# Attention with a sign-weight feed-forward: other places for the feed-forward's pieces, and one more product of ones in the first batch

## The chip, the core and the metric

The kernel runs on one core of a Trainium2 chip. Its engines work at the same time, each through its own list of instructions in order: TensorE (PE: matmuls and transposes, PEld: its loads of stationary weights), VectorE (DVE), ScalarE (ACT), GpSimd (POOL) and SyncE (SP, which here only issues DMAs). TensorE writes to PSUM, which is used as eight banks of 128 x 512 floats. The metric is the device time of one execution in microseconds. Before the change it is 4385.95 us, the median of three runs (4385.45 to 4386.15).

## The reference, cut to what matters

`x` is 4 batches of 2048 rows of 512 floats. There are 16 heads of 32 columns each.

```python
x = L0_attn_x
q, k, v = x @ Wq.T, x @ Wk.T, x @ Wv.T               # by head: (4, 16, 2048, 32)
attn = softmax(q @ k.T / sqrt(32), axis=-1)          # per head: 2048 x 2048
x = _layernorm(x + attn @ v)
w = where(weights >= 0, 1, -1)
y = clip((x @ w.T) * scale + bias, -100, 100)        # the feed-forward
x = _layernorm(x + y)
```

## The kernel before, in words

**Tiling.** Four heads (128 columns) are worked on together as one group: `n` counts the 16 groups, four per batch (`b, g = divmod(n, 4)`; `NG` is 4). In a group, `qb` counts four blocks of 512 queries (`NQB`), and `kc` counts 16 chunks of 128 keys (`NT`). One pair of block and chunk is one **step**: 64 steps per group (`STEPS`), 1024 steps in all (`total`). Batch 0 is the groups 0 to 3, and so on. I number steps of a group from 0 to 63; "step 11" without more means step 11 of the 16 steps of a block.

**One step on TensorE**, in this order:

- `scores`: for each of the four heads, a matmul that adds minus the row maximum (L300, bf16, with the tile `negm`) and one of keys by queries (L306), into four banks. ScalarE takes exp of the four banks into a tile `p` (L313), which comes from the pool `ppool` with four buffers.
- `max_unit`: queries by keys (L248) for a block 22 steps ahead (`LEAD`), into four banks. VectorE takes row maxima of three banks straight from PSUM; ScalarE copies the fourth to `moved` first. In the step named in `ahead` (step 11) VectorE also finishes the maxima of a block in `max_parts` (L280 to L284), between the first and second row maximum.
- **fillers**, from a plan (below).
- on even steps, `weighted`: exp times values for the two steps before (L324), which VectorE adds to `oT`.

GpSimd adds up the tiles `p` of a block in `acc` (`add_up`, L344): one addition for `kc` 1 to 14. When the block is over, `denominators` sums over keys with a matrix of ones (`ones_times`, L350): once with the last `p` (`kc` 15) and once with `acc`. The last block of all is treated otherwise (`is_last`).

**Fillers.** The order of all work is written out by the program that builds the kernel. `at(step, f)` puts a call at the end of a step (`behind`). `task(kind, first, last, f)` hands a piece of TensorE work to the planner, which places it between `first` and `last`:

- "big", on odd steps, at most two units of weight: `project_v` (a piece of values, weight 1), `project_k` and `project_q` (a piece of keys or queries, twice as wide, weight 2; all L206), and `ffn` (a third of the feed-forward of a tile of 128 rows, L532, weight 1, which VectorE works on in three instructions, L537, L538 and L540);
- "small", on odd steps: `transpose_x` (L195), `turn` (transposes of a normalised tile, L518) and `add_attention` (L391, two VectorE instructions on 512 columns);
- "col", on even steps: `denominators`.

`plan` walks through the steps. It takes the pieces whose `last` is near (`must`), then others (`can`) by their order of `last`. It runs twice: first as early as possible, to count how much weight falls in each group (`used`); then with these counts as `quota`, holding each group to its running share. A step is `heavy` when it is in `ahead` or has an `add_attention`; it then gets no third by choice, and no limit from the share. If one unit is allowed, a piece of values is preferred; if two, a third with a piece of values, or one wide piece.

**The feed-forward of a batch** runs beside the attention of the next. `finish(b, qb, a, every, w, lag)` sets its places for a block of 512 rows: load the rows (SP), statistics per tile of 128 rows (VectorE), `rstd` (a power on GpSimd) and `shift` (ScalarE), then for each of the four tiles, `every` steps apart, `norm` (ScalarE), a task `turn`, three tasks `ffn`; at last the second normalisation and the store (SP). `every` is 13 for the feed-forward of batches 0 and 1 and 11 for that of batch 2. That of batch 3 is placed by `finish_last` and `finish_end`, which are not touched.

Of the kernel before, what the change touches and what calls it, by code (L numbers as in the profile page):

```python
# [20 lines left out]
def kernel(  # L21
# [41 lines left out]
    kpool = ctx.enter_context(tc.tile_pool(name="kpool", bufs=2))  # L63
    qpool = ctx.enter_context(tc.tile_pool(name="qpool", bufs=3))
    vpool = ctx.enter_context(tc.tile_pool(name="vpool", bufs=2))
    ppool = ctx.enter_context(tc.tile_pool(name="ppool", bufs=4))
    apool = ctx.enter_context(tc.tile_pool(name="apool", bufs=2))
    work = ctx.enter_context(tc.tile_pool(name="work", bufs=2))
    once = ctx.enter_context(tc.tile_pool(name="once", bufs=1))
# [223 lines left out]
    def is_last(n, qb):  # L293
        return n == B * NG - 1 and qb == NQB - 1
# [22 lines left out]
    def weighted(pair):  # L317
# [18 lines left out]
            nc.vector.tensor_tensor(outs[n, qb], pb, outs[n, qb], ALU.add)  # L336
        give(b, "DVE", 0.6)

    def add_up(n, qb, kc, p, before):
        if kc == 1:  # L340
            acc[n, qb] = apool.tile([P, HG, QB], F32, tag="acc", name="acc")
        if 0 < kc < (NT // 2 if is_last(n, qb) else NT - 1):
            a = acc[n, qb]
            nc.gpsimd.tensor_tensor(a, before if kc == 1 else a, p, ALU.add)  # L344
        if kc == NT - 1:
            last_p[n, qb] = p

    def ones_times(b, p, start, stop):
        for h in range(HG):
# [17 lines left out]
    def denominators(n, qb):  # L367

        if is_last(n, qb):
            b = sums[0]  # L370
        else:
            b = take()
            ones_times(b, last_p.pop((n, qb)), True, False)
            whole = acc.pop((n, qb))
            ones_times(b, whole, False, True)
        if is_last(n, qb):
            dT = mpool.tile([P, QB], F32, tag="moved", name="dT")
        else:
# [195 lines left out]
    def at(step, f, *args):  # L574
        behind[step].append(lambda: f(*args))
# [2 lines left out]
        tasks[kind].append((last, first, len(tasks[kind]), f, args, after, gap))  # L578
        return kind, len(tasks[kind]) - 1

    def finish(b, qb, a, every, w, lag):
        f = Finish(b, qb)
        at(a, f.load)
        for j in range(NTQ):
            at(a + 2 + j, f.stats, 1, j)
        at(a + 6, f.rstd, 1)
        at(a + 7 + lag, f.shift, 1)
        for j in range(NTQ):
            t = a + 8 + lag + every * j
            at(t, f.norm, 1, j)  # L590
            turned = task("small", t + 1, t + 3, f.turn, j)
            for k in range(3):
                task("big", t + 2, t + w, f.ffn, j, k, after=turned)
            at(t + w, f.stats, 2, j)
        e = a + 9 + lag + every * (NTQ - 1) + w
        at(e, f.rstd, 2)
        at(e + 1 + lag, f.shift, 2)
        for j in range(NTQ):
            at(e + 2 + lag + j, f.norm, 2, j)
        at(e + 5 + lag, f.store)  # L600

    def finish_last(qb, last):

# [56 lines left out]
    for n in range(N):  # L660
        b, g = divmod(n, NG)
        s0 = n * STEPS
        ready = [s0 - STEPS + 1] * NQB
        for i in range(NQB):
            if g:
                break
            first = start if n == 0 else s0 - STEPS + (2, 10, 20, 31)[i]
            last = -LEAD + NTQ * i - (2 if i else 6) if n == 0 else first + (12, 12, 11, 8)[i]
            for j in range(NTQ):
                turned[b, i, j] = task("small", first, last, transpose_x, b, i, j)  # L670
            ready[i] = first
        def latest(i, s):

            return min(s, s0 + (0, 9, 19, 30)[i]) if g == NG - 1 else s

        for t in range(NT):
            i, j = divmod(t, NTQ)
            after = turned[b, i, j]
            task("big", max(s0 - STEPS + 2, ready[i], -6), latest(i, s0 + t), project_v, n, t,
                 after=after)  # L680
            if j % 2 == 0:
                continue
            free = s0 - STEPS + 1 if n else start
            task("big", max(free, ready[i]), s0 - LEAD - 1 + i * (1 if n else NTQ),
                 project_k, n, t // 2, after=after)
            last = s0 + NT * i - LEAD + NTQ * (j - 1) - 1
            if n == 0 and i == 0:
                last = -LEAD - 2 + j
            task("big", max(s0 + NT * (i - 2), start), latest(i, last), project_q, n, t // 2,
                 after=after)  # L690
        for qb in range(NQB):
            first = s0 + NT * qb
            last = first + NT - 1
            ahead[first - 5] = n, qb
            at(last + 2, load_columns, n, qb)
            w = 0 if n == N - 1 else 6
            d = last + 2 if is_last(n, qb) else last + 3
            t = task("col", d, d + w, denominators, n, qb)
            if is_last(n, qb):
                t = task("small", d + 1, d + 1, reciprocals, n, qb, after=t)  # L700
                task("small", d + 2, d + 2, add_attention, n, qb, after=t)
            else:
                task("small", d + 3, d + 4 + w, add_attention, n, qb, after=t, gap=3)
            if g == NG - 1:
                if b < B - 1:
                    every = 13 if b < B - 2 else 11
                    finish(b, qb, (b + 1) * NG * STEPS + qb * (5 * every - 1), every, every, 3)
                else:
                    (finish_end if is_last(n, qb) else finish_last)(qb, last)

# [6 lines left out]
    def plan(quota=None):  # L717

        gone = {kind: set() for kind in tasks}
        done, steps, used = {}, defaultdict(list), defaultdict(int)  # L720

        def may(kind, s):
            some = (t for t in tasks[kind] if t[1] <= s and t[2] not in gone[kind])
            return [t for t in some if t[5] is None or done.get(t[5], s) + t[6] <= s]

        s = start
        while any(len(gone[kind]) < len(tasks[kind]) for kind in tasks):
            middle = 0 <= s < total
            soon = s + 2 if 0 <= s + 1 < total else s + 1
            group, at_n = divmod(s, STEPS)  # L730
            if not middle:
                most = {"col": 1, "small": 1, "big": 1}
            elif s % 2:
                most = {"small": 1, "big": 2}
            else:
                most = {"col": 1}
            heavy = s in ahead
            for kind in most:
                some = sorted(may(kind, s))
                must = [t for t in some if t[0] < soon]  # L740
                can = [t for t in some if t[0] >= soon]
                k = most[kind]
                if kind == "small" and middle and len(some) > 3:
                    k = 2
                if kind == "big" and s < 0 and len(some) > 1 and some[1][0] <= s + 4:
                    k = 2
                if kind == "big":
                    if middle and quota is not None and not heavy:
                        k = max(1, min(k, -(-quota[group] * (at_n + 1) // STEPS) - used[group]))


                    thirds = [t for t in can if on_vector(t)]
# [24 lines left out]
            s += 1  # L777
        return steps, used
# [86 lines left out]
```

## Time and profile before

| what | value |
|---|---|
| median of the runs | 4385.95 us |
| the profiled execution | 4386.25 us, of which the span of instructions is 4384.5 us |
| first step begins / last step begins | 84.4 us / 4329.0 us |
| batch 0 (groups 0 to 3) | 1031.7 us |
| groups 4 to 7 | 267.2, 265.6, 265.6, 272.6 us |
| groups 8 to 11 | 266.3, 265.4, 265.7, 272.7 us |
| groups 12 to 15 | 267.2, 269.9, 269.4, 265.3 us |
| granted TensorE clock | 0.998 |
| an addition on GpSimd (L344) | 4.54 us, 825 with `acc` and 64 that begin one |

The times of groups are read off the starts of their first L300 matmuls in the timeline; groups 7 and 11 also turn `x` of the next batch.

How to read the lines that follow: the page gives for each engine its busy time, its share of the span and its number of instructions. The chain of waits, followed back from the last instruction, says which engine's work set the end. A line of waits reads "who <- whom: us in total, times, longest us". A line of the timeline reads start, duration, engine, line of the kernel, operation, output and inputs, shape and how many in a row; a bracket at its end gives the idle time before it and what ended it.

### The profile page before, as it was taken

How to read it: one execution, taken by the hardware profiler on the slowest of the kernel's cores; microseconds unless marked ns; L12 is line 12 of the kernel's file. 1: busy time of each engine (PE TensorE's matmuls, PEld its weight loads, DVE VectorE, ACT ScalarE, POOL GpSimd, SP SyncE). 2: the span in 40 equal slices, each digit the busy share in tenths (PEclk: the TensorE clock that was granted, in tenths of full speed). 3: DMA queues.
4: the chain of work that ended last, by engine and by line, in shares of the span. 5: the costliest groups of instructions: out<-in, count | busy, mean ns of one | idle time of the engine just before them, and what ended most of it. 6: DMA issues, size and time to landing. Idle time of an engine off the chain costs nothing.

```text
span 4384.5 us, 89302 instructions
## 1 busy us (share of the span) xinstructions
PE 4345.0 (99%) x36092; PEld 2135.5 (49%) x36092; DVE 3315.9 (76%) x5908; ACT 2999.3 (68%) x6173; POOL 4083.3 (93%) x940
## 2 busy tenths in 40 slices
PE   9999999999999999999999999999999999999998
PEld 5444444444454454455445454455544545455443
DVE  6777777777777777777777777777777777777774
ACT  4666666676667667676676766767667676767665
POOL 3999999999999999999999999999999999999993
PEclk9999999999999999999999999999999999999999
DMA  2000000010001000011000100001100000001101
GB/s 88 11 10 14 11 14 10 12 39 22 21 13 27 13 23 20 11 45 36 21 20 11 33 10 21 23 10 49 25 20 21 20 21 23 20 11 33 24 23 49
DMA packets 263351, 101.41 MB, mean 23 GB/s; under 512 B 169372, under 2 KB 239004, under 8 KB 262936
## 3 DMA queue, kind: packets, MB, share of 16 engines
q1 hardware_dynamic: 257656, 91.50, 8.6%
q8 instruction: 282, 4.62, 0.4%
q10 hardware_dynamic: 5280, 4.19, 0.3%
q14 instruction: 133, 1.09, 0.1%
HBM read 54.26 MB, written 33.02 MB: 20 GB/s over the span
## 4 chain that ended last, share of the span: by engine, by line
PE 91%; POOL 6%; DVE 1%; ACT 1%; issue 1%; DMA 0%; ACTq 0%; POOLq 0%; DVEq 0%
PE ps L324 20%; PE ps L248 19%; PE ps L306 19%; PE ps L206 15%; PE ps L300 8%; POOL acc L344 6%; PE ps L532 5%; PE ps L350 3%; PE ps L391 1%; PE ps L195 1%; PE ps L518 1%; ACT p L313 1%; DVE part L255 1%; DMA xs<-in_L_attn_x_dram 0%; PE ps L139 0%
## 5 line engine op out<-in xcount | busy, mean ns | idle before, releaser
L344 POOL TENSOR_TENSOR acc<-acc,p 128x2048 f32<-128x2048 f32 x825 | 3743.7, 4538 | 102.8 <-ACT p L313 42.6
L313 ACT ACTIVATE p<-ps 128x512 f32<-128x512 f32 x4096 | 2114.8, 602 | 1136.0 <-PE ps L306 1108.2
L255 DVE TENSOR_REDUCE part<-ps 128x1 f32<-128x512 f32 x3072 | 1933.0, 683 | 774.6 <-PE ps L248 774.2
L248 PE MATMUL ps<-kT,qT 32*128 32x512 f32 x8192 | 1114.3, 590 | 0.2 <-DVE xg_last L434 0.2
L306 PE MATMUL ps<-qT,kT 32*128 32x512 f32 x8192 | 1073.3, 591 | 0.0
L324 PE MATMUL ps<-p,vv 128*32 128x512 f32 x8192 | 983.4, 598 | 1.8 <-ACT p L313 1.8
L248 PEld LDWEIGHTS ps<-kT,qT 32*128 32x128 f32 x8192 | 542.8, 184 | 381.0 <-issue 194.5
L255 DVE TENSOR_REDUCE part<-moved 128x1 f32<-128x512 f32 x1024 | 691.9, 676 | 3.3 <-ACT moved L267 3.2
L267 ACT COPY moved<-ps 128x512 f32<-128x512 f32 x1024 | 631.0, 616 | 22.1 <-PE ps L248 18.0
L324 PEld LDWEIGHTS ps<-p,vv 128*32 128x32 f32 x8192 | 220.2, 109 | 686.9 <-issue 345.9
L300 PE MATMUL ps<-negm,ones_bf 32*128 32x512 bf16 x4096 | 443.1, 384 | 4.9 <-ACT p L313 2.9
L306 PEld LDWEIGHTS ps<-qT,kT 32*128 32x128 f32 x8192 | 405.8, 184 | 44.3 <-issue 27.5
L336 DVE TENSOR_TENSOR oT<-ps,oT 128x512 f32<-128x512 f32 x448 | 309.7, 691 | 97.4 <-PE ps L324 59.2
L344 POOL TENSOR_TENSOR acc<-p 128x2048 f32<-128x2048 f32 x64 | 290.8, 4544 | 96.0 <-ACT p L313 95.8
L300 PEld LDWEIGHTS <-ones_bf 32*128 32x128 bf16 x4096 | 105.6, 91 | 551.0 <-issue 522.3
L206 PEld LDWEIGHTS ps<-wvT,xT 128*128 128x128 f32 x2048 | 250.9, 191 | 80.3 <-ACT p L313 75.6
L206 PE MATMUL ps<-wvT,xT 128*128 128x128 f32 x2048 | 279.2, 280 | 0.3 <-ACT p L313 0.2
L206 PE MATMUL ps<-xT,wqT 128*128 128x256 f32 x1024 | 248.8, 386 | 2.7 <-ACT p L313 2.7
L206 PE MATMUL ps<-xT,wkT 128*128 128x256 f32 x1024 | 248.7, 387 | 0.0
L206 PEld LDWEIGHTS ps<-xT,wkT 128*128 128x128 f32 x1024 | 184.9, 190 | 68.8 <-ACT p L313 47.0
L206 PEld LDWEIGHTS ps<-xT,wqT 128*128 128x128 f32 x1024 | 184.5, 190 | 66.6 <-ACT p L313 44.9
L532 PEld LDWEIGHTS ps<-wsT,nT 128*128 128x128 f32 x1152 | 167.8, 189 | 94.2 <-ACT p L313 93.3
(75 smaller groups left out, 1722.4 us busy)
## 6 DMA issues: line engine op xcount, KB each, us to landing
xs<-in_L_attn_x_dram SPq DMA_DIRECT2D x64, 256.0 KB
xc<-in_L_attn_x_dram SPq DMA_DIRECT2D x60, 256.0 KB
res<-xc SPq DMA_DIRECT2D x60, 256.0 KB
xg<-res SPq DMA_DIRECT2D x12, 1024.0 KB
out_dram<-xg SPq DMA_DIRECT2D x12, 1024.0 KB
xg_last<-res SPq DMA_DIRECT2D x4, 768.0 KB
out_dram<-xg_last SPq DMA_DIRECT2D x3, 1024.0 KB
raw_wk<-in_L_attn_Wk_dram ACTq DMA_DIRECT2D x4, 256.0 KB
```

What stands on the lines that cost most here:

```text
L206: nc.tensor.matmul(pp, lhsT=lhs(c), rhs=rhs(c), start=(c == 0), stop=(c == DC - 1))
L248: nc.tensor.matmul(ps[:, banks[h], :], lhsT=qT[n, qb][rows, ts(qc, P)], rhs=kT[n][rows, ts(kb, QB)], start=True, stop=True,)
L255: nc.vector.tensor_reduce(part[:, qc, h : h + 1, kb], src, AX.X, ALU.max, negate=True)
L267: nc.scalar.copy(moved, ps[:, banks[-1], :])
L300: nc.tensor.matmul(ps[:, banks[h], :], lhsT=ones_bf[rows, :], rhs=negm[n, qb][rows, :], start=True, stop=False,)
L306: nc.tensor.matmul(ps[:, banks[h], :], lhsT=kT[n][rows, ts(kc, P)], rhs=qT[n, qb][rows, :], start=False, stop=True,)
L313: nc.scalar.activation(p[:, h, :], ps[:, banks[h], :], AF.Exp, scale=SM_SCALE)
L324: nc.tensor.matmul(pb[cols, :], lhsT=vv[n][:, kc, cols], rhs=p[:, h, :], start=(i == 0), stop=(i == 1),)
L336: nc.vector.tensor_tensor(outs[n, qb], pb, outs[n, qb], ALU.add)
L344: nc.gpsimd.tensor_tensor(a, before if kc == 1 else a, p, ALU.add)
L350: nc.tensor.matmul(ps[h * HD : (h + 1) * HD, b, :], lhsT=ones, rhs=p[:, h, :], start=start, stop=stop,)
L532: nc.tensor.matmul(py, lhsT=self.nT[j][:, c, :], rhs=wT["ws"][:, c, cols], start=(c == 0), stop=(c == DC - 1),)
```

## The change

- `ppool` has five buffers in place of four.
- In batch 0 (`n < NG`) GpSimd adds the chunks 1 to 13, and `denominators` multiplies ones with the last two tiles `p` and with `acc`: three products in place of two.
- `finish` takes the step `t0` of the first `norm`. For the feed-forward of batches 0 and 1 the tiles are 16 steps apart (`even`), the `norm` is at step 8, the `turn` at step 11 exactly, and the thirds have to be done by 15 steps after the `norm`; for that of batch 2 the tiles are 12 steps apart and the blocks 53. The statistics and the second normalisation have other places.
- `plan` takes the share as a number, not rounded up: under 1.25 it allows one unit, but not in heavy steps nor where a third and a piece of values are both there. Of the pieces of values it keeps back as many as thirds come up in the next six steps. Two thirds may be chosen together.

```diff
-    ppool = ctx.enter_context(tc.tile_pool(name="ppool", bufs=4))
+    ppool = ctx.enter_context(tc.tile_pool(name="ppool", bufs=5))
...
+    def chunks_added(n, qb):
+
+        if is_last(n, qb):
+            return NT // 2
+        return NT - 2 if n < NG else NT - 1
+
...
-        if 0 < kc < (NT // 2 if is_last(n, qb) else NT - 1):
+        if 0 < kc < chunks_added(n, qb):
             a = acc[n, qb]
             nc.gpsimd.tensor_tensor(a, before if kc == 1 else a, p, ALU.add)
-        if kc == NT - 1:
-            last_p[n, qb] = p
+        elif kc >= NT - 2:
+            last_p[n, qb] = last_p.get((n, qb), []) + [p]
...
-            ones_times(b, last_p.pop((n, qb)), True, False)
+            for k, p in enumerate(last_p.pop((n, qb))):
+                ones_times(b, p, k == 0, False)
...
-    def finish(b, qb, a, every, w, lag):
+    def finish(b, qb, t0, every):
+
         f = Finish(b, qb)
-        at(a, f.load)
+        even = every == NT
+        at(t0 - 24, f.load)
+        for j, t in enumerate((t0 - 17, t0 - 15, t0 - 9, t0 - 5)):
+            at(t, f.stats, 1, j)
+        at(t0 - 5, f.rstd, 1)
+        at(t0 - 2, f.shift, 1)
         for j in range(NTQ):
-            at(a + 2 + j, f.stats, 1, j)
-        at(a + 6, f.rstd, 1)
-        at(a + 7 + lag, f.shift, 1)
+            t = t0 + every * j
+            at(t, f.norm, 1, j)
+            turned = task("small", t + 3 if even else t + 1, t + 3, f.turn, j)
+            by = t + every - 1 if even else t + every
+            for k in range(3):
+                task("big", t + 2, by, f.ffn, j, k, after=turned)
+            at(by, f.stats, 2, j)
+        e = by
+        at(e, f.rstd, 2)
+        at(e + 4, f.shift, 2)
         for j in range(NTQ):
-            t = a + 8 + lag + every * j
-            at(t, f.norm, 1, j)
-            turned = task("small", t + 1, t + 3, f.turn, j)
-            for k in range(3):
-                task("big", t + 2, t + w, f.ffn, j, k, after=turned)
-            at(t + w, f.stats, 2, j)
-        e = a + 9 + lag + every * (NTQ - 1) + w
...
+            at(e + 5 + j, f.norm, 2, j)
+        at(e + 8, f.store)
...
-                    every = 13 if b < B - 2 else 11
-                    finish(b, qb, (b + 1) * NG * STEPS + qb * (5 * every - 1), every, every, 3)
+                    every, apart = (NT, STEPS) if b < B - 2 else (12, 53)
+                    finish(b, qb, (b + 1) * NG * STEPS + 8 + apart * qb, every)
...
-                    if middle and quota is not None and not heavy:
-                        k = max(1, min(k, -(-quota[group] * (at_n + 1) // STEPS) - used[group]))
+                    due = 2 if quota is None or not middle else (
+                        quota[group] * (at_n + 1) / STEPS - used[group]
+                    )
...
+                    if middle:
+
+                        next_thirds = sum(
+                            on_vector(t) and t[1] <= s + 6 and t[2] not in gone[kind]
+                            for t in tasks[kind]
+                        )
+                        spare = max(len(values) - next_thirds, 1 if thirds else 0)
+                        values = values[:spare]
...
+                    if middle and due < 1.25 and not heavy and not (thirds and values):
+                        k = 1
...
-                        can = wide[:1] or values[:2] or thirds[:1]
+                        can = wide[:1] or values[:2] or thirds[:2]
```

More of the change, by code (lines that the diff above doesn't have):

```diff
@@ L579, in task @@
         return kind, len(tasks[kind]) - 1
-    def finish(b, qb, a, every, w, lag):
+    def finish(b, qb, t0, every):
         f = Finish(b, qb)
-        at(a, f.load)
-        for j in range(NTQ):
-            at(a + 2 + j, f.stats, 1, j)
-        at(a + 6, f.rstd, 1)
-        at(a + 7 + lag, f.shift, 1)
-        for j in range(NTQ):
-            t = a + 8 + lag + every * j
-            at(t, f.norm, 1, j)
-            turned = task("small", t + 1, t + 3, f.turn, j)
-            for k in range(3):
-                task("big", t + 2, t + w, f.ffn, j, k, after=turned)
-            at(t + w, f.stats, 2, j)
-        e = a + 9 + lag + every * (NTQ - 1) + w
[L596 to L600, printed above, removed]
+        even = every == NT
[4 more added lines that the diff above has]
+        at(t0 - 2, f.shift, 1)
+        for j in range(NTQ):
+            t = t0 + every * j
[8 more added lines that the diff above has]
+        at(e + 4, f.shift, 2)
+        for j in range(NTQ):
+            at(e + 5 + j, f.norm, 2, j)
+        at(e + 8, f.store)
     def finish_last(qb, last):
```

## The prediction

> **What bounds the kernel now.** I read the page first (engines, chain), then the waits of the first batch, then TensorE's timeline step by step.
>
> ```profile
> span 4384.5 us, 89302 instructions
> PE 4345.0 (99%) x36092; PEld 2135.5 (49%) x36092; DVE 3315.9 (76%) x5908; ACT 2999.3 (68%) x6173; POOL 4083.3 (93%) x940
> PE 91%; POOL 6%; DVE 1%; ACT 1%; issue 1%; DMA 0%; ACTq 0%; POOLq 0%; DVEq 0%
> ACT p L313 <- POOL acc L344: 17.8, 11, 2.1
> ```
>
> The last line is from the waits between 84 and 1120 us (the first batch). TensorE is the path; GpSimd, though 93% busy, is on it only in the first batch, where exp waits for buffers of p that the additions still read. A busy share of 99% hides short waits, so I read TensorE's timeline. The first matmuls of a step (L300) start it; I call an odd step with the even one behind it a pair, and its price is the time from its L300 to the second next L300. Three pairs, each with its filler line and the L300 lines around it:
>
> ```profile
> 1179.96 0.39 PE L300 MATMUL ps<-negm,ones_bf 32*128 32x512 bf16 x4
> 1182.00 1.16 PE L206 MATMUL ps<-wvT,xT 128*128 128x128 f32 x8
> 1183.09 0.69 PE L300 MATMUL ps<-negm,ones_bf 32*128 32x512 bf16 x4
> 1187.29 0.39 PE L300 MATMUL ps<-negm,ones_bf 32*128 32x512 bf16 x4
> ...
> 1496.14 0.40 PE L300 MATMUL ps<-negm,ones_bf 32*128 32x512 bf16 x4
> 1498.18 1.99 PE L206 MATMUL ps<-xT,wkT 128*128 128x256 f32 x8
> 1501.19 1.36 PE L248 MATMUL ps<-kT,qT 32*128 32x512 f32 x8
> 1504.34 0.39 PE L300 MATMUL ps<-negm,ones_bf 32*128 32x512 bf16 x4
> ...
> 969.90 0.39 PE L300 MATMUL ps<-negm,ones_bf 32*128 32x512 bf16 x4
> 971.94 0.65 PE L195 MATMUL ps<-ident,xs 128*128 128x128 f32 x4
> 972.43 1.94 PE L206 MATMUL ps<-xT,wkT 128*128 128x256 f32 x8
> 978.20 0.39 PE L300 MATMUL ps<-negm,ones_bf 32*128 32x512 bf16 x4
> ```
>
> First: a lone piece of values, 7.33 us. Other fillers leave 5.94 us for scores, maxima and weighted sums (a piece of keys or queries 7.87, less 1.82 to 1.93; a third beside a piece of values 8.18, less 1.25 and 0.99), so this pair waits 7.33 - 5.94 - 0.99 = 0.40 us: the next step's matmuls come late. Second: step 11 of 16, where VectorE finishes the row maxima (L280 to L284, 1.1 us): 8.21 instead of 7.87, the 0.34 lying in L248's 1.36 us. Third: also step 11, with a turn of x (four transposes) beside the keys: 8.30. Outside step 11 a turn and a wide piece (keys or queries) cost 8.30 too. So transposes at step 11 cost 0.09 us, elsewhere 0.43: they lie in the wait.
>
> **The change part by part.** Prices are pair prices from that timeline; a pair's wait is its price less 5.94 and less its fillers (a turn 0.49).
>
> (1) A third ones-product (L350) per block in batch 0, 16 in all. The two of now raise a pair from 7.87 to 9.58 and from 8.18 to 9.91, 0.87 each: 16 x 0.87 = +13.9 us on TensorE, with nothing to hide it.
>
> (2) 16 fewer additions there (4.54 us each, plus 0.07 between two). GpSimd now needs 14 x 4.61 = 64.5 us per 16 steps, where the groups take 63 to 66; after, 59.9. What it costs now: six pairs with queries and the two ones-products are above 9.58: 10.67, 10.94, 10.78, 10.84, 10.94, 10.26, together 6.95 over; two pairs without filler take 7.65 and 7.66 where a third takes 6.99: 1.33. Sum -8.3. In the first such pair, exp's 1.55 us wait for GpSimd shows ahead of L350. Bounds: nothing, and the 17.8 us of all exp's waits. I take 8.3, since it is TensorE's own time. Batch 0: +5.6. Its order stays: the share is met in steps of 1.5 there, so that `due` is 1.0 or 1.5 and both rules pick one or two alike (group 0 differs in a few steps, same count of lone values).
>
> [...]
>
> (3) A tile per 16 steps in batches 1 and 2, turned at step 11, thirds at 13, 15, 1. I followed the new rule by hand through group 5. Before: 11 thirds beside values, 1 beside queries (10.72 with two ones-products, so 9.0 without), 4 lone values, 1 value with a turn (7.44), 3 turns with wide pieces, 4 wide pieces at step 11, 4 with add_attention, 4 others. After: 12 thirds beside values; lone values at 3 (twice, after the ones-products, 7.27) and once elsewhere (7.33); 3 turns with wide pieces at step 11; the fourth turn there with a value; 9 plain wide pieces. So lone values do not vanish: 16 values less 12 thirds leave 4. The fourth turn should cost 8.21, not 7.44: a step 11 with no filler at all, late in the kernel, takes 8.23, so the pair has a floor. Before, without the unchanged: 3 x 8.30 + 7.44 + 4 x 8.21 + 4 x 7.87 + 4 x 7.33 + 9.0 + 11 x 8.18 = 225.0. After: 3 x 8.30 + 8.21 + 9 x 7.87 + 2 x 7.27 + 7.33 + 12 x 8.18 = 224.0. That is -1.0 per group. The statistics of rows leave the steps with add_attention, where 10 pairs with keys cost 8.47 instead of 8.32: -0.15. Two odd pairs (8.51 and 8.71 with a third and a value) in groups 4 and 8: -0.9. Six groups: 6 x -1.15 - 0.9 = -7.8. Unknown are both ends of the step-11 floor (7.44 to 8.23) and whether thirds right after step 11 stay at 8.2; 21 of 24 pairs at 13 do, and 18 with ones-products at 1 are all at 9.89 or 9.91.
>
> (4) Groups 7 and 11 (x of the next batch is turned too). Now: lone values 4 x 0.40, a lone third 0.80 (7.99), two thirds 0.54 (8.98), a step 11 of 0.40: 3.3 us of waits. After, by hand: one turn of x alone 0.90 (as 7.33 for a turn alone), a lone value 0.34, a turn with a value at step 11 0.79: 2.0. So -1.3 each, -2.6.
>
> (5) Batch 3, a tile per 12 steps in place of 11. By hand, waits of groups 12 to 15 (5.3, 5.6, 3.4 and what group 15 has to step 29, 14.0) become 4.4, 4.8, 1.7 and 11.2: fewer lone values, add_attention at step 5 beside queries (8.32 with or without them), against it an empty step 11 and some turns alone. -6.2, the weakest number: nothing to -9.
>
> (6) At nothing: the fifth buffer of p only loosens; the two last p live until the ones-products at step 2, and with five buffers the exp of step 3 waits only for the first of these. The 1 MB loads of rows are issued on SP 24 steps ahead of the first tile, stores 8 steps behind the last; the buffer wanted was stored over 30 steps earlier, so the sums and transposes queued behind on SP do not wait. rstd's power (0.92 us on GpSimd) stands behind one or two additions in line, and shift reads it 3 or 4 steps (12 us and more) later; if GpSimd were later than that, ScalarE's queue, exp first, would wait. Norms move among steps where ScalarE has 5.4 us of exp and moved copies in a pair of 8.
>
> Sum: +5.6 - 7.8 - 2.6 - 6.2 = -11.0 on this execution's own 4386.25 us (span 4384.5 and 1.75 around it): 4375.3. The median, 4385.95, is 0.3 lower: 4375.
>
> **The rivals.** (a) The parts cancel: -11 shrinks to between -8 and +6, because batch 3 gives nothing and the fourth turn and groups 7 and 11 find other waits: +5.6 - 7.8 + 0 = -2, 4384. For it: most pairs are only reshuffled, and the count of lone values stays. Against: the turn at step 11 is a row, 8.30 three times.
> (b) Slower: VectorE becomes the bound, with the row maxima at step 11 and thirds at 13, 15 and 1. Price per tile between 0.3 and 0.99 (a third and a value at step 11 cost 9.17, not 8.18; a lone third 0.80). With 32 tiles and 0.8: 4375 + 25.6 = 4401. It decides above 19.8/32 = 0.62 us per tile. Against: VectorE has 5.44 + 0.69 us of maxima and sums in a pair, 7.2 with a third, below 8.18, and 21 of 24.
> (c) More: GpSimd's hold on the first batch was worth all 17.8 us, -9.5 further: 4366. For it: the 6% of the chain. Against: TensorE's own pairs show 8.3.
>
> **How the numbers follow.** A difference under 0.2% (8.8 us) can hardly be told from none here. Forecast (-9 to -16) 0.45, (a) 0.36, (b) 0.09, (c) 0.10. So faster 0.54, same 0.37, slower 0.09. Range: (c) with a little more of batch 3 gives 4364; (a) with none of (3) to (5) 4386 + 5.6 less a little, 4390. The likeliest alone: 4370 to 4377.
>
> **What would show it.** L350 with p goes from 568 to 696 matmuls (16 products of 8); L344 with acc from 825 to 809; exp's wait for GpSimd in batch 0 goes; pairs with queries and three ones-products take 10.45; step 11 with turn and keys 8.30, with L248 back at 1.03; plain groups 264.5 instead of 265.6; batch 0 about 1037 instead of 1031.7. I am wrong if pairs at 13 rise above 8.3, if batch 0 gets shorter, or if ScalarE waits for rstd.

## The result and the profile after

The change made the kernel slightly slower. The median went from 4385.70 us (12 runs) to 4396.78 us (12 runs, 4394.04 to 4398.78); the ratio is 1.0024, with a 95% interval from 1.0017 to 1.0032. I had predicted 4375, with a range to 4390. The profiled execution took 4398.19 us, 1.8 us of it outside the span. The page of the kernel after, its span, its engines and its chain of waits:

```profile
span 4396.4 us, 89443 instructions
PE 4353.7 (99%) x36220; PEld 2136.6 (49%) x36220; DVE 3321.6 (76%) x5908; ACT 3000.4 (68%) x6173; POOL 4012.3 (91%) x924
PE 95%; DVE 2%; ACT 2%; issue 0%; DMA 0%; POOL 0%; ACTq 0%; DVEq 0%
```

GpSimd has gone from the chain (6% before). VectorE and ScalarE went from 1% to 2% each, and that is already the hint: TensorE waits at some places for a chain that runs through both. Where these places are shows as soon as the span is cut by batches, at the starts of the first L300 matmuls in TensorE's timeline:

| stretch | before | after | difference | predicted |
|---|---|---|---|---|
| batch 0 | 1031.7 | 1037.2 | +5.5 | +5.6 |
| batches 1 and 2 | 2141.1 | 2135.1 | -6.0 | -10.4 |
| batch 3 | 1071.8 | 1084.4 | +12.6 | -6.2 |
| ahead of the first step, and from the last on | 139.9 | 139.7 | -0.2 | 0 |

So the first term came out nearly to the tenth, the second at a bit over half, and the third with the wrong sign and twice its size. To be explained is batch 3.

Its waits give the place. These are ScalarE's waits for VectorE over the whole span, "who <- whom: us in total, times, longest us"; first the kernel before:

```profile
ACT ve L488 <- DVE mv L483: 20.7, 9, 8.5
```

and the same line of the program in the kernel after, over the span and then between 3250 and 4340 us, which is batch 3:

```profile
ACT ve L495 <- DVE mv L490: 48.7, 32, 8.6
...
ACT ve L495 <- DVE mv L490: 17.1, 11, 3.4
```

This is the first instruction of `rstd`: ScalarE adds epsilon to the variance that VectorE has just written (`mv`, from `bn_aggr`). It waited 9 times before; now it waits 32 times. Pair by pair, the dear ones of batch 3 are those in which it waits: pair 877 takes 11.43 us instead of 7.97, 931 takes 11.43 instead of 7.87, 983 takes 11.97 instead of 8.51. (I number pairs by their odd step over all 1024; batch 3 begins at 768.) The timelines of ScalarE, VectorE and TensorE in pair 877:

```profile
3722.41 0.62 ACT L267 COPY moved<-ps 128x512 f32<-128x512 f32 x1
3725.61 0.30 ACT L495 ACTIVATE ve<-mv,eps_t 128x4 f32<-128x4 f32 x1 [2.58 <-DVE mv L490]
3726.40 0.30 ACT L495 ACTIVATE ve<-mv,eps_t 128x4 f32<-128x4 f32 x1 [0.50 <-DVE mv L490]
3726.60 2.04 ACT L313 ACTIVATE p<-ps 128x512 f32<-128x512 f32 x4
```

```profile
3724.08 0.68 DVE L255 TENSOR_REDUCE part<-moved 128x1 f32<-128x512 f32 x1
3724.67 0.68 DVE L489 BATCH_NORM_STATS2 st<-xg 128x6 f32<-128x512 f32 x1
3725.39 0.18 DVE L490 BATCH_NORM_AGGREGATE mv<-st 128x2 f32<-128x6 f32 x1
3725.49 0.66 DVE L489 BATCH_NORM_STATS2 st<-xg 128x6 f32<-128x512 f32 x1
3726.18 0.18 DVE L490 BATCH_NORM_AGGREGATE mv<-st 128x2 f32<-128x6 f32 x1
```

```profile
3722.53 0.45 PE L300 MATMUL ps<-negm,ones_bf 32*128 32x512 bf16 x4
3722.75 1.08 PE L306 MATMUL ps<-qT,kT 32*128 32x512 f32 x8
3723.61 1.72 PE L248 MATMUL ps<-kT,qT 32*128 32x512 f32 x8
3727.23 3.41 PE L324 MATMUL ps<-p,vv 128*32 128x512 f32 x16 [1.90 <-ACT p L313]
3730.57 0.55 PE L300 MATMUL ps<-negm,ones_bf 32*128 32x512 bf16 x4
```

Read them together. ScalarE is free at 3723.03 us. The next exp could begin soon after: its scores (L306) run from 3722.75. But ahead of exp in ScalarE's queue stand two `rstd`, of two different blocks of rows, in the same step. They wait for two sets of statistics, and these stand behind the row maxima in VectorE's queue, one after the other. So exp begins at 3726.60, and the weighted sum (L324), which needs exp, leaves TensorE idle for 1.90 us. Two instructions of 0.30 us have held up the path.

The last of these lines shows a second loss: sixteen L324 matmuls take 3.41 us instead of 1.92. The granted clock says why. The stretch around it as a row of the windows view (start:end, us, busy time of PE, PEld, DVE, ACT, POOL, then the granted clock, the DMA share and GB/s):

```profile
3717.00:3732.00 15.00, 13.10 (x99) 5.16 (x98) 11.12 (x21) 7.69 (x17) 14.84 (x6) 0.89 0.00 1
```

The mean clock is 0.89 here. In the records it falls to half (0.50) for 3.41 us three times in the kernel after where it doesn't before, at 3727.5, 3952.8 and 4178.1 us, each time within 2 us of the end of such a gap, in the pairs 877, 931 and 983. I call such a stretch at half clock a dip. The other executions of the kernel after are not all alike in this: six of the twelve, the profiled one among them, have a mean granted clock of 0.996 and take 4397.5 to 4398.8 us, the six with 0.997 or 0.998 take 4394.0 to 4396.1 us. So the profiled one is probably among those with more dips.

### The profile page after: what moved, and what is told of

It is laid out like the page before. It is cut to its first block, busy times and chain, and to the rows that moved or that the text cites. A ratio compares the mean times of both kernels' runs of the same rounds, so it can differ in the third digit from the quotient of the medians.

```text
span 4396.4 us, 89443 instructions
## 1 busy us (share of the span) xinstructions
PE 4353.7 (99%) x36220; PEld 2136.6 (49%) x36220; DVE 3321.6 (76%) x5908; ACT 3000.4 (68%) x6173; POOL 4012.3 (91%) x924
## 4 chain that ended last, share of the span: by engine, by line
PE 95%; DVE 2%; ACT 2%; issue 0%; DMA 0%; POOL 0%; ACTq 0%; DVEq 0%
PE ps L324 21%; PE ps L248 20%; PE ps L306 20%; PE ps L206 16%; PE ps L300 8%; PE ps L539 5%; PE ps L356 3%; DVE part L255 1%; ACT p L313 1%; PE ps L398 1%; PE ps L195 1%; PE ps L525 1%; DVE st L489 0%; PE ps L139 0%; DMA raw_wk<-in_L_attn_Wk_dram 0%
## 5 line engine op out<-in xcount | busy, mean ns | idle before, releaser
L350 POOL TENSOR_TENSOR acc<-acc,p 128x2048 f32<-128x2048 f32 x809 | 3671.7, 4539 | 114.3 <-ACT p L313 56.8
L248 PE MATMUL ps<-kT,qT 32*128 32x512 f32 x8192 | 1099.4, 589 | 2.2 <-ACT p L313 2.1
L306 PE MATMUL ps<-qT,kT 32*128 32x512 f32 x8192 | 1073.1, 592 | 0.0
L324 PE MATMUL ps<-p,vv 128*32 128x512 f32 x8192 | 985.9, 599 | 5.7 <-ACT p L313 5.1
L248 PEld LDWEIGHTS ps<-kT,qT 32*128 32x128 f32 x8192 | 534.8, 185 | 378.0 <-issue 184.2
L324 PEld LDWEIGHTS ps<-p,vv 128*32 128x32 f32 x8192 | 220.4, 109 | 692.2 <-issue 343.2
L300 PE MATMUL ps<-negm,ones_bf 32*128 32x512 bf16 x4096 | 443.4, 385 | 5.8 <-ACT p L313 3.0
L306 PEld LDWEIGHTS ps<-qT,kT 32*128 32x128 f32 x8192 | 406.2, 184 | 40.6 <-issue 22.8
L300 PEld LDWEIGHTS <-ones_bf 32*128 32x128 bf16 x4096 | 107.2, 91 | 557.9 <-issue 528.9
```

What stands on the lines that cost most here:

```text
L248: nc.tensor.matmul(ps[:, banks[h], :], lhsT=qT[n, qb][rows, ts(qc, P)], rhs=kT[n][rows, ts(kb, QB)], start=True, stop=True,)
L300: nc.tensor.matmul(ps[:, banks[h], :], lhsT=ones_bf[rows, :], rhs=negm[n, qb][rows, :], start=True, stop=False,)
L306: nc.tensor.matmul(ps[:, banks[h], :], lhsT=kT[n][rows, ts(kc, P)], rhs=qT[n, qb][rows, :], start=False, stop=True,)
L324: nc.tensor.matmul(pb[cols, :], lhsT=vv[n][:, kc, cols], rhs=p[:, h, :], start=(i == 0), stop=(i == 1),)
```

## The experiments

**The theory (A).** In the new `finish`, `rstd` is put in the very step of the last statistics that it reads: `at(t0 - 5, f.stats, 1, 3)` and `at(t0 - 5, f.rstd, 1)`, and likewise `at(by, f.stats, 2, j)` and `at(e, f.rstd, 2)` with `e = by`. Before, both stood one step later. **The rivals**: the places of the tiles in batch 3 themselves (12 steps apart) are bad there; or the planner's new rule is, with VectorE as the bound behind step 11.

### `rstd` one step later

```diff
-        at(t0 - 5, f.rstd, 1)
-        at(t0 - 2, f.shift, 1)
+        at(t0 - 4, f.rstd, 1)
+        at(t0 - 1, f.shift, 1)
...
-        at(e, f.rstd, 2)
+        at(e + 1, f.rstd, 2)
```

> The changed kernel with both rstd one step later, so that ScalarE's first instruction of rstd (L495) no longer stands in the same step as the last statistics that it reads. Theory A (ScalarE waits for VectorE's statistics, exp waits behind it, TensorE runs dry, at four places in batch 3 and a little at 16 in batches 1 and 2): the pairs at 825, 877, 931 and 983 of 9.32, 11.43, 11.43 and 11.97 us fall to 7.3 to 8.2, batch 3 loses 10 to 16 us, batches 1 and 2 lose 2 to 5 (pairs of 8.16 at steps 3 and 7 back at 7.87); 4376 to 4385. Rival B (the thirds and values of batch 3 stand badly: lone thirds, empty steps, four wide pieces): nothing moves by more than 2 us, 4395 to 4398.

Measured: 4382.47 us (10 runs, 4381.67 to 4384.97), beside 4386.03 for the kernel before on the same chip; ratio 0.9992 (0.9983 to 1.0001). That is not clear of the kernel before. Against the kernel after it is 14.3 us less (14.6 when each is taken against the kernel before beside it), from three calls moved by a step, and inside the range that I expected. Batch 3 takes 1072.1 us instead of 1084.4, batches 1 and 2 take 2131.8 instead of 2135.1. The waits of the kernel with `rstd` later, over the whole span, and ScalarE's timeline at the same place in the program as above:

```profile
ACT ve L495 <- DVE mv L490: 21.3, 9, 8.5
```

```profile
3717.12 0.62 ACT L267 COPY moved<-ps 128x512 f32<-128x512 f32 x1
3718.57 2.06 ACT L313 ACTIVATE p<-ps 128x512 f32<-128x512 f32 x4 [0.84 <-PE ps L306]
3720.97 0.53 ACT L495 ACTIVATE ve<-mv,eps_t 128x4 f32<-128x4 f32 x2
```

Exp now stands ahead of the two `rstd`, waits only for its own scores, and the two follow without a wait, since the statistics are a step old. Pair 877 is at 7.97 again. The same stretch in the windows view of this kernel:

```profile
3717.00:3732.00 15.00, 15.00 (x124) 6.06 (x122) 12.48 (x25) 9.81 (x22) 12.94 (x5) 1.00 0.01 1
```

TensorE is busy throughout at a clock of 1.00, where it had 13.10 of 15 us at 0.89. The three dips are gone: the clock is 1.00 here, from 3942 to 3961 and from 4166 to 4187 us too.

### The kernel before with `rstd` early

The reverse, in the kernel before and with nothing else of the change.

```diff
-        at(a + 6, f.rstd, 1)
+        at(a + 5, f.rstd, 1)
...
-        at(e, f.rstd, 2)
+        at(e - 1, f.rstd, 2)
```

> The kernel before, in which both rstd of finish stand one step earlier, in the step of the last statistics; nothing else moves. Theory A: waits of ScalarE for the statistics appear where there were none (24 places, large where a third ends in the same step), 4 to 14 us more than before: 4390 to 4400. Rival B: same as before within 2 us, 4384 to 4388.

Measured: 4409.31 us (4 runs, 4408.67 to 4410.05); ratio 1.0051 (1.0035 to 1.0068), so 23 us slower, more than I expected. The batches 1 to 3 take 1077.8, 1078.3 and 1080.0 us instead of 1071.0, 1070.1 and 1071.8. Its waits over the whole span, and one of them on ScalarE in batch 1:

```profile
ACT ve L488 <- DVE mv L483: 66.5, 33, 8.3
```

```profile
1413.79 0.30 ACT L488 ACTIVATE ve<-mv,eps_t 128x4 f32<-128x4 f32 x1 [1.40 <-DVE mv L483]
1414.00 2.04 ACT L313 ACTIVATE p<-ps 128x512 f32<-128x512 f32 x4
```

The cause works alone, and at the same mean clock as in the kernel before (0.998 in both profiles). I had expected less because I thought of it at the places of the new plan; in the old plan `rstd` meets other neighbours: pairs at step 5 with add_attention (VectorE has more to do there) go from 8.47 to 9.65, those at step 63 from 7.33 to 8.16. The wait is 1.4 us at both places in most groups; why it costs 1.18 us at one and 0.83 at the other isn't shown.

### Which of the two `rstd`

Two kernels with one execution each: only the second normalisation's `rstd` later (`at(e + 1, f.rstd, 2)`), and only the first's (`t0 - 4`, with its shift at `t0 - 1`).

> The changed kernel with only the second rstd of each block one step later; the first stays in the step of its last statistics. In batch 3 the second rstd of one block and the first of the next stand in the same step (824, 877, 930), behind the same VectorE work, so theory A expects the pairs at 825, 877 and 931 to keep most of their waits (at most 1.2 us less each) and only 983, where one stands alone, to fall to about 8.5; batch 3 at 1077 to 1081 instead of 1084.4. If each rstd costs its own share, batch 3 falls by half or more of the 12 us, to 1078 or less, spread over all four places.

> The changed kernel with only the first rstd of each block one step later. Theory A: 983 unchanged near 12 us, 825, 877 and 931 at most 1.2 us less each, batch 3 at 1080 to 1084; in batches 1 and 2 the pairs at step 3 fall from 8.16 to 7.87 and those at step 7 stay.

Batch 3 took 1081.7 us with the second later and 1078.9 with the first later, so 2.7 and 5.5 less than 1084.4; both together give 12.3. They don't add because in the pairs 877 and 931 both stand in one step, the blocks of rows being 53 steps apart there: with only the second moved, these pairs stay at 11.54 and 11.42; with only the first moved, they fall to 9.15 and 9.00; with both to 7.97 and 7.87. The fall to 9.15 and 9.00 is 2.3 and 2.4 us, where I had expected 1.2 at most. Most of it is the clock: over the four stalls of batch 3 (3490 to 3510, 3717 to 3732, 3942 to 3961 and 4166 to 4187 us) the kernel with only the first later is at a clock of 1.00 throughout, the one with only the second later still has three dips (0.91, 0.89 and 0.91 in the first three of these stretches). Moved alone the first also did harm: its shift came into the step of the second `rstd`, pairs at step 7 rose to 9.14, and batches 1 and 2 became longer by 2.3 and 2.4 us.

These two kernels also price a dip, since waits stayed where dips moved. Pair 983 has the first `rstd` later and the second early in one of them: it stalls there as in the kernel after, without the dip. Windows of the kernel after, and of the one with the first later, over that stall:

```profile
4166.00:4187.00 21.00, 18.91 (x124) 8.34 (x124) 15.92 (x31) 10.44 (x23) 20.84 (x7) 0.92 0.00 1
```

```profile
4166.00:4187.00 21.00, 18.91 (x133) 8.72 (x132) 18.53 (x36) 12.02 (x26) 20.76 (x7) 1.00 0.00 1
```

TensorE is idle for the same 2.09 us in both, but in 3.4 us at half clock it gets fewer matmuls done (124 to 133). The pairs 983 and 985 take 11.97 and 10.07 with the dip, 11.04 and 9.35 without: 1.65 us, about half of 3.4. Pair 825, with the dip only in the kernel with the second later, says 1.53 (10.85 to 9.32). So of batch 3's 12.3 us some 5 are the three dips (an estimate, 3 x 1.65), and the other 7 the waits themselves. By the same price nearly all of the 5.5 us that the first one gave alone are the dips.

### Two ones-products again

The kernel after with `chunks_added` as it was:

```diff
-        return NT - 2 if n < NG else NT - 1
+        return NT - 1
```

> The changed kernel with two products of ones and 14 additions per block in batch 0 again, five buffers kept. The prediction's sum (13.9 us for 16 products against 8.3 us of waits for GpSimd): 5.6 us less in batch 0, 4391. Rival C (the fifth buffer alone took most waits for GpSimd): up to 13.9 less, 4383. Rival D (GpSimd's hold costs more than 13.9): 4397 or more.

And its counterpart, the kernel before with five buffers and three products in batch 0, nothing else:

```diff
-    ppool = ctx.enter_context(tc.tile_pool(name="ppool", bufs=4))
+    ppool = ctx.enter_context(tc.tile_pool(name="ppool", bufs=5))
...
-        if 0 < kc < (NT // 2 if is_last(n, qb) else NT - 1):
+        if 0 < kc < (NT // 2 if is_last(n, qb) else NT - 2 if n < NG else NT - 1):
...
-        if kc == NT - 1:
-            last_p[n, qb] = p
+        elif kc >= NT - 2:
+            last_p[n, qb] = last_p.get((n, qb), []) + [p]
...
-            ones_times(b, last_p.pop((n, qb)), True, False)
+            for k, p in enumerate(last_p.pop((n, qb))):
+                ones_times(b, p, k == 0, False)
```

> The kernel before with three products of ones and 13 additions per block in batch 0, and five buffers of p; the old places and the old rule of the share. The prediction's sum: batch 0 5.6 us longer, the rest unchanged, 4391.5. Rival D: 4386 or less.

Measured: 4391.6 us (10 runs, ratio to before 1.0013, 1.0003 to 1.0022), and 4391.11 us (10 runs, ratio 1.0009, 1.0000 to 1.0019). Batch 0 is 1030.3 us in the first and 1037.1 in the second: in the kernel after, the third product cost 6.9 there (1037.2 to 1030.3); together with the fifth buffer it cost 5.4 over the kernel before. What the difference of 1.5 is, the next experiment tells.

### Five buffers alone

The kernel before with `bufs=5` as its only edit, one execution.

> The kernel before with five buffers of p and nothing else. The prediction: a buffer only loosens, exp's waits for GpSimd (21.1 us in all) shrink, but over batch 0 GpSimd's 64.5 us per 16 steps stay the pace where they are; batch 0 0 to 2 us shorter than 1031.7, the rest unchanged. Rival C: batch 0 shorter by 5 us or more, which would make the third product needless as a remedy.

Batch 0: 1030.4 us, 1.3 less than before. Its waits between 84 and 1120 us, for GpSimd's sum:

```profile
PEld ps L350 <- POOL acc L344: 10.0, 7, 2.7
PE ps L350 <- POOL acc L344: 5.2, 4, 1.8
ACT p L313 <- POOL acc L344: 2.5, 2, 1.4
```

Exp's 17.8 us are down to 2.5. But the ones-products now wait for the same GpSimd, which they didn't before: the matmuls for 5.2 us, the loads of their weights for 10.0. These two waits run at the same time (at the place below the loads wait 2.33 us and the matmuls 1.42), so they aren't to be added. A place where it can be seen, TensorE's timeline in pair 129:

```profile
608.13 1.07 PE L350 MATMUL ps<-p,ones 128*32 128x512 f32 x8
610.62 1.06 PE L350 MATMUL ps<-acc,ones 128*32 128x512 f32 x8 [1.42 <-POOL acc L344]
```

The buffer didn't make GpSimd faster (an addition takes 4.54 us in the kernel before and, with five buffers, in the kernel after), so the wait went to the next one that needs the sum. That is why the extra product, which does relieve GpSimd, had something left to earn: four pairs of batch 0 with five buffers and two products are above 9.58 (11.21, 10.77, 10.83 and 11.55), 6.0 us together. And it is why that was still not enough. Of the 16 products 15 lie in the steps of batch 0, the last in group 4: 15 x 0.87 = 13.1 us of TensorE for 6.4 (13.1 less the 6.7 between 1037.1 and 1030.4).

### `rstd` later and two ones-products

Both of these edits in the kernel after.

> The changed kernel with both rstd one step later and two products of ones in batch 0 again. If the two causes add up (rstd 14.3 us, products 5.3 us): batch 0 at 1030, batches 1 and 2 at 1067 and 1065, batch 3 at 1072; 4377, that is 9 us less than the kernel before. Rival: the products' additions on GpSimd delay rstd's power and shift, 4380 or more.

Measured: 4373.2 us (7 runs, 4372.66 to 4374.35), beside 4385.29 before; ratio 0.9973 (0.9962 to 0.9984). Batch 0 is 1030.1, batches 1 and 2 are 1066.0 and 1064.7, batch 3 is 1072.5. It is faster than both kernels, 12.1 us less than the one before. Each batch is within 1 us of what I expected; the total of 4377, made from differences of medians, was 4 us too high.

### The places alone, the rule alone

Two halves of the change, each in the kernel before: the new places for the feed-forward of batches 0 and 1 (tiles 16 steps apart, `turn` at step 11, `rstd` a step later), with the old planner; and the new `plan` with the old places.

```diff
-                    every = 13 if b < B - 2 else 11
-                    finish(b, qb, (b + 1) * NG * STEPS + qb * (5 * every - 1), every, every, 3)
+                    if b < B - 2:
+                        finish_even(b, qb, (b + 1) * NG * STEPS + 8 + STEPS * qb, NT)
+                    else:
+                        finish(b, qb, (b + 1) * NG * STEPS + qb * 54, 11, 11, 3)
```

```diff
-                    if middle and quota is not None and not heavy:
-                        k = max(1, min(k, -(-quota[group] * (at_n + 1) // STEPS) - used[group]))
+                    due = 2 if quota is None or not middle else (
+                        quota[group] * (at_n + 1) / STEPS - used[group]
+                    )
...
+                        next_thirds = sum(
+                            on_vector(t) and t[1] <= s + 6 and t[2] not in gone[kind]
+                            for t in tasks[kind]
+                        )
+                        spare = max(len(values) - next_thirds, 1 if thirds else 0)
+                        values = values[:spare]
...
+                    if middle and due < 1.25 and not heavy and not (thirds and values):
+                        k = 1
...
-                        can = wide[:1] or values[:2] or thirds[:1]
+                        can = wide[:1] or values[:2] or thirds[:2]
```

> The kernel before with only the new places for the feed-forward of batches 0 and 1 (a tile per 16 steps, the turn at step 11, rstd one step after the statistics); the old rule of the share, the old batch 3, two products, four buffers. Theory E (the gain of batches 1 and 2 comes from the turns at step 11, 0.34 us for each with a wide piece, and from statistics away from add_attention): batches 1 and 2 together 5 to 10 us shorter than before, 4376 to 4381. Rival F (the gain comes from the rule that keeps values for the thirds): less than 2 us, 4384 to 4388.

> The kernel before with only the new rule of the planner (share not rounded up, values kept for coming thirds, two thirds together); all places, products and buffers as before. Theory E: batches 1 and 2 within 3 us of before, since 16 values and 12 thirds per group leave four lone values under either rule; 4383 to 4389. Rival F: 5 to 10 us less there.

Measured: 4380.18 us (10 runs; ratio 0.9988, 0.9979 to 0.9997) for the places, 4379.32 us (10 runs; 0.9986, 0.9977 to 0.9995) for the rule. In batches 1 and 2 they give 5.9 and 5.8 us. Together, with `rstd` later, batches 1 and 2 give 9.3, and 10.4 with two products as in these two kernels. That is 1.3 to 2.4 less than the sum of 11.7. But the profiles of the two kernels that leave these batches as they were (five buffers alone, three products with five buffers) are 1.8 and 1.2 us shorter there than that of the kernel before, so whether the two gains are in part the same isn't shown. My expectation that the rule would do little on the old places was wrong: in group 5 it leaves two lone values (7.27 and 7.33) and puts two beside turns (7.50 and 7.44), which have next to no wait, where the old rule had four lone ones and one beside a turn.

### The turn left free

The kernel with `rstd` later and two products, but `turn` from step 9 on instead of step 11 exactly:

```diff
-            turned = task("small", t + 3 if even else t + 1, t + 3, f.turn, j)
+            turned = task("small", t + 1, t + 3, f.turn, j)
```

> The kernel of e5_later_two with the turn of an even tile allowed from one step after its norm, so that it falls at step 9 and not at step 11. Theory E: per group three turns with wide pieces cost 0.34 us more, and the one with a value, free of the floor of step 11, 0.4 less; batches 1 and 2 together 3 to 6 us longer than in e5_later_two. If step 11 does not hide the turn: no difference within 1.5 us.

Measured: 4382.64 us (10 runs; ratio 0.9994, 0.9985 to 1.0003), and batches 1 and 2 cost 8.3 us more than with the turn at 11, more than the 3 to 6 that I expected. The six plain groups take 1595.8 us, as in the kernel before (1595.7). The value that I thought would be free of the floor isn't: alone at step 11 it takes 8.20 or 8.21 too. TensorE's timeline of this kernel, the steps 9 and 11 of a block (which end at 1425.33 and 1433.54 with their even steps):

```profile
1417.07 0.39 PE L300 MATMUL ps<-negm,ones_bf 32*128 32x512 bf16 x4
1419.12 0.66 PE L525 MATMUL ps<-ident,xg 128*128 128x128 f32 x4
1419.61 1.89 PE L206 MATMUL ps<-xT,wkT 128*128 128x256 f32 x8
1425.33 0.40 PE L300 MATMUL ps<-negm,ones_bf 32*128 32x512 bf16 x4
1427.37 2.00 PE L206 MATMUL ps<-xT,wkT 128*128 128x256 f32 x8
1430.39 1.37 PE L248 MATMUL ps<-kT,qT 32*128 32x512 f32 x8
1433.54 0.39 PE L300 MATMUL ps<-negm,ones_bf 32*128 32x512 bf16 x4
```

Beside it the same turn in the kernel after, at step 11:

```profile
1499.77 0.39 PE L300 MATMUL ps<-negm,ones_bf 32*128 32x512 bf16 x4
1501.81 0.66 PE L525 MATMUL ps<-ident,xg 128*128 128x128 f32 x4
1502.30 1.94 PE L206 MATMUL ps<-xT,wkT 128*128 128x256 f32 x8
1505.26 1.03 PE L248 MATMUL ps<-kT,qT 32*128 32x512 f32 x8
1508.07 0.39 PE L300 MATMUL ps<-negm,ones_bf 32*128 32x512 bf16 x4
```

At step 9 the turn makes a pair of 8.26 us, and step 11 still takes 8.21, with L248 drawn out to 1.37 us while VectorE finishes the maxima. At step 11 the pair with the turn takes 8.30, and L248 is at 1.03: the transposes lie in time that was lost there anyhow.

### The shifts apart

Batch 3 had promised -6.2 us, and with `rstd` later it is only level with before. At 881 (10.43 us, 9.81 before) the shifts of two blocks fall into one step: ScalarE's timeline of the kernel with `rstd` later has ten short instructions, 2.0 us, ahead of exp:

```profile
3734.20 0.21 ACT L504 ACTIVATE neg<-rs 128x4 f32<-128x4 f32 x1
3734.44 0.85 ACT L508 ACTIVATE nb<-mv,neg 128x1 f32<-128x1 f32 x4
3735.20 0.19 ACT L504 ACTIVATE neg<-rs 128x4 f32<-128x4 f32 x1
3735.42 0.86 ACT L508 ACTIVATE nb<-mv,neg 128x1 f32<-128x1 f32 x4
3736.18 2.02 ACT L313 ACTIVATE p<-ps 128x512 f32<-128x512 f32 x4
```

So, on the kernel with `rstd` later and two products, the first shift a step earlier:

```diff
-        at(t0 - 1, f.shift, 1)
+        at(t0 - 2, f.shift, 1)
```

> The kernel of e5_later_two with the first shift of each block two steps before its first norm, not one. In batch 3 the blocks are 53 steps apart, so that in e5_later_two the shift of one block's second normalisation and that of the next block's first fall in one step (828, 881, 934) and put ten short ScalarE instructions, 2.1 us, ahead of the exps. Apart, the pairs behind them (829 at 8.10, 881 at 10.42, 935 at 8.61) lose 0.4 to 1 us each; batch 3 1 to 3 us shorter, 4370 to 4373. If the power on GpSimd is not done by then, ScalarE waits for it and nothing is gained.

Measured: 4374.06 us (8 runs, 4373.43 to 4376.21); ratio 0.9972 (0.9961 to 0.9983), the same as without it, and batch 3 at 1072.4 instead of 1072.5, where I had expected 1 to 3 us less. Pair 881 did fall, from 10.42 to 9.63, 829 from 8.10 to 7.53 and 935 from 8.61 to 8.25, together 1.7 us; but 827, into which the moved shift now falls, rose from 8.21 to 8.70. The rest went at places that the edit doesn't touch: 1007 rose from 13.56 to 13.95 (it is 12.91 in the kernel with three products, whose batch 3 has the same code), and three pairs by 0.2 each. The lump of two shifts isn't what keeps batch 3 from its gain, or not by itself.

## Why the prediction was wrong

**(1) and (2), the third product and GpSimd: right.** Batch 0 is +5.5, predicted +5.6. The pair of the timeline that I named, queries and three ones-products, takes 10.44 us in the kernel after, predicted 10.45:

```profile
607.22 0.40 PE L300 MATMUL ps<-negm,ones_bf 32*128 32x512 bf16 x4
613.23 1.92 PE L356 MATMUL ps<-p,ones 128*32 128x512 f32 x16
614.97 1.04 PE L356 MATMUL ps<-acc,ones 128*32 128x512 f32 x8
617.66 0.39 PE L300 MATMUL ps<-negm,ones_bf 32*128 32x512 bf16 x4
```

The price had been read off TensorE's own pairs, not off exp's 17.8 us of waits; both experiments on the third product (5.4 over the kernel before, 6.9 in the kernel after) fit it. GpSimd's 93% was worth no more than that. The shares were not as predicted, though: I had put the fifth buffer at nothing and all of the gain to the additions, and the buffer alone gave 1.3 us, the additions 6.4. One of the six dear pairs (10.26) and one product lie in group 4, so in batch 0 the sum is 13.1 - 1.3 - 6.4 = 5.4.

**(3), the turn at step 11: the mechanism right, the size too large.** The plan followed by hand is what the kernel does in five of the six plain groups (5, 6, 8, 9, 10; group 4 has another order); the step-11 pair is 8.30 as predicted, and taking the place away costs 8.3 us. The six became 3.6 us shorter (1595.7 to 1592.1), where -7.8 was predicted; with `rstd` later it is 6.3. So 2.7 of the missing 4.2 us are the failed step (6) below, and 1.5 stay. About as much is one row that the sum had wrong: a wide piece alone at step 57, counted at 7.87 us, takes 8.20 in each of the five groups (5 x 0.33 = 1.65), with L248 drawn out to 1.36 us there as at step 11. A plain group then takes 264.5 us (groups 8 to 10), the number on record; in the kernel after it takes 265.1.

**(4), groups 7 and 11: right.** -2.4 us for both, predicted -2.6.

**(5), batch 3: wrong.** Predicted -6.2, measured +12.6. Of that, 12.3 go with `rstd` (1084.4 to 1072.1). What is left, +0.3, is still 6.5 off. I had counted the waits of groups 12 to 14 and of group 15 up to step 29 as 4.4, 4.8, 1.7 and 11.2; with `rstd` later they are about 7.5, 4.9, 3.9 and 10.9. So two of the four counts, those of groups 12 and 14, were too low by 2 to 3 us. Group 15 behind step 29, which wasn't in the count, is no part of it: it takes 134.4 us instead of 134.6 (pair 1007 rose from 11.62 to 12.91 because it got a third from 1009, which fell from 8.45 to 7.28). In group 12 a pair without any filler takes 8.10 us (829) and a lone third 7.97, twice. I had followed TensorE's fillers there by hand, but not the pieces on ScalarE (shift, norm) which in batch 3, with blocks 53 steps apart, meet in the same steps. The one of these that I took apart gave nothing, so how much of the 6.5 each holds is open.

**(6), "at nothing": the step that failed.** I had put `rstd` at nothing; where it stands costs 15.6 us (12.3 in batch 3 and 3.3 in batches 1 and 2), some 5 of them by the clock. I looked at `rstd` and followed its second instruction, the power on GpSimd, into `shift`, and named ScalarE's queue as what would suffer. Its first instruction is on ScalarE itself and reads VectorE's statistics, and I didn't look up the step in which these are made. The line of the diff shows it: `f.stats, 1, 3` and `f.rstd, 1` have the same `t0 - 5`. The condition that I had put down myself, "if ScalarE waits for rstd", came true in a shorter way than I meant. It could have been estimated from rows of before: a statistic is 0.68 and 0.18 us on VectorE (L482, L483), so one set that comes behind a row maximum of 0.68 us ends up to 1.5 us later, two sets 2.4. Even that would have been too little for batch 3. In the kernel after the waits are 1.0 us at most in batches 1 and 2 (15 of them, 12.6 us, of which 3.3 reach the path), and 2.6 to 3.4 us in four pairs of batch 3 (825, 877, 931, 983), in three of which two `rstd` stand in one step.

**The rivals.** (b) had the sign right and the mechanism wrong: pairs at step 13 stay at 8.20, so VectorE isn't the bound. What made the kernel slower is a wait through VectorE's queue, at some steps of each block of rows, dear in four pairs of batch 3, and not at 32 tiles. (a) had batch 3 giving nothing; that is what the kernel with `rstd` later shows, and it ends at 4382.5 where (a) said 4384. (c) fell with batch 0.

**The clock.** I had no term for it, and some 5 us of batch 3 are its. What the runs show of it stands at the end.

## What to carry to other kernels

A tiny instruction that reads another engine's result belongs a step behind that result: here 0.3 us that waited 3 us held up what was queued behind on ScalarE, exp, and with it TensorE. When a schedule is rewritten, list for each moved call every instruction that it issues, on which engine, and the step in which its input is made; do so first for those that look free. And a wait that a buffer removes is not gone until one knows who waits next for the same engine.

## What was not expected of the hardware

Behind gaps of 1.85 to 2.09 us on TensorE the granted clock stood at half (0.50) for 3.41 us, at 1.5 to 1.65 us of lost time each. The trace has the start of each dip: 3727.526, 3952.805 and 4178.085 us in the kernel after, and 3500.858, 3726.137 and 3951.417 in the one with only the second `rstd` later. The distances are 225.279 or 225.280 us in both. In the clock record of the kernel after, each of its three dips lasts 3.413 us, and the stretches at full clock between them 221.866 us, 65 times as long; the stretches behind the third, up to the last one at half clock, last 95.573, 6.827, 81.920, 6.827 and 13.653 us (28, 2, 24, 2 and 4 times). What sets these lengths no run shows.

The length of a gap alone doesn't decide whether a dip follows. The gap at 983 (2.09 us, from 4174.09 to 4176.18) was followed by one in the kernel after; with only the first `rstd` later the same 2.09 us were followed by none (a clock of 1.00 from 4166 to 4187 us), nor was the gap of 1.11 us at 877 there (1.00 from 3717 to 3732). The gap of 1.86 us at 825 in the kernel after (3500.31 to 3502.17) brought no dip (1.00 from 3490 to 3510), while the same gap was followed by one in the kernel with the second `rstd` later (0.91 over the same stretch). What else decides is open.
